# A two-layer expert network in which the first matmul runs as 26 block products in place of 28, with weight forms kept in memory and the second weight streamed

## The chip, the core and the metric

The kernel runs on one core of a Trainium2 chip. The core has a matrix engine (TensorE, PE in the profile, with the loading of its stationary operand as PEld), a vector engine (Vector, DVE), an activation engine (Scalar, ACT), a general engine (GpSimd, Pool) and a queue engine that issues transfers (SyncE, SP). Each takes its instructions in the order in which the program wrote them, and waits at one whose inputs are not ready. Sums are built in PSUM, which TensorE writes and Vector and Scalar read; all else lies in SBUF, and the inputs and outputs in DRAM. The metric is the time on the device in microseconds.

## What is computed

There are 2 sequences of 2048 tokens of width 512. First comes an adapter, then a feed-forward layer with an expert chosen per sequence. Cut to what matters (all in 32-bit floats, with the biases and both layer norms):

```python
# adapter: 512 -> 128 -> (expert 128x128, embedding) -> 512, residual, layer norm
hidden = gelu(x @ down_W.T + down_b)
hidden = hidden @ expert_W[e0].T + expert_b[e0] + domain_emb[e0]
x = layernorm(hidden @ up_W.T + up_b + x) * ln_gamma + ln_beta
# expert feed-forward: 512 -> 2048 -> 512, residual, layer norm
h = gelu(x @ Wi[e1] + bi[e1])          # Wi: 512 x 2048
r = h @ Wo[e1] + bo[e1] + x            # Wo: 2048 x 512
out = layernorm(r) * gamma[e1] + beta[e1]
```

## The kernel before

The work is cut into 8 blocks `n` of 512 tokens; blocks 0 to 3 are the first sequence, `b = 0`, and 4 to 7 the second. The program runs a block as two stages. Stage F (`f_in`, line 467) computes `h` from the adapter's transposed output `yT`; stage G (`f_out`, line 595) computes the second matmul into `x_tiles[n]`. The adapter of block n+1 is woven into G of block n by `adapter_pieces` (line 426). The program order is written by hand: `f_in` and `f_out` call `hook()` after each group of matmuls, and the lists `F[i]` and `G[i]`, filled in the loop from line 811, say which other work is put at hook i. A hook gives only the place in each engine's own queue; an engine whose queue is empty runs ahead of TensorE.

**Stage F.** Both layers use a 2x2 block scheme of seven products in place of eight (the Winograd form of Strassen's). The columns of Wi go in four tiles `d`. For each, TensorE multiplies seven forms of Wi (A11, A12, A22 and the sums S1 to S4) by seven forms of `yT` (four raw blocks, one of them replaced by a sum, and `t1`, `t2`, `t4`). A product is 4 matmuls of 128x128 by 128x256, so F has 4 x 7 x 4 = 112 (block 0 runs its first tile plainly with 32 in place of 28). Results are copied out by Scalar (`snap`, line 524), added by Vector (line 530) and passed through the gelu on Scalar (line 482). There are 28 hooks, 7 for a tile.

**Weights.** `load_wi` (line 270) loads raw Wi for the first block of a sequence, `sums_wi` (line 282) makes S1 to S4 on Pool, and `keep_wi` (line 292) writes the made tile, 1.79 MB, to DRAM; the other blocks load it from there. Two tiles are in flight. `load_wo` (line 298) loads all of Wo of a sequence at once, and `sums_wo` (line 307) makes its forms on Pool in four calls of four sums; raw Wo and the sums stay in SBUF for all four blocks.

**Stage G.** Seven products again, each of 32 matmuls over eight k; X and Y begin with six of their eight k (12 matmuls each). In hook 0 stands `a_xT` (line 442), in which Vector turns the loaded squares `xs` of the next block's x into `xT`; in hook 1 stands the adapter's first matmul, `a_down` (its matmul is line 372, tile `pdown`). Later hooks hold `a_up`, `a_norm`, the moves of 32x32 squares `ys` (line 111), the transposes into `yT` (line 447), the bias addition `a_bo` on Pool and the sums of `yT` (`a_sums`, line 412, on Vector). Sums of `h` (`h_s13`, `h_s2`, `h_s4`) run on Vector.

**The end of a block.** Layer norm of block n-1 runs in F of block n: `f_moments` and `f_rstd`, then `f_normalize` on Vector at hooks 7, 8, 14 and 15, and `f_store` three hooks later. At hook 19 `load_x` and `load_squares` fetch block n+1; there are two x buffers, so this load waits until the last store of block n-1 has landed. All these transfers are issued by SP, in order:

```python
F[7 * d + 6].append(lambda m=m: (load_wi(*m), sums_wi(*m)))
(F[7 * d + 12] if d + 1 < ND else G[5]).append(lambda m=m: keep_wi(*m))
...
F[i + 3].append(lambda s=s: f_store(n - 1, s))
...
F[19].append(lambda: (load_x(n + 1), load_squares(n + 1)))
```

Of the kernel before, what the change touches and what calls it, by code (L numbers as in the profile page):

```python
# [9 lines left out]
F32 = mybir.dt.float32  # L10
# [3 lines left out]
PSUM = bass.MemoryType.PSUM  # L14


@with_exitstack
def kernel(
# [32 lines left out]

    nc = tc.nc
    P = 128
# [21 lines left out]
    wo_pool = ctx.enter_context(tc.tile_pool(name="wo", bufs=1))  # L75
# [3 lines left out]
    pre_pool = ctx.enter_context(tc.tile_pool(name="pre", bufs=6))  # L79
    small = ctx.enter_context(tc.tile_pool(name="small", bufs=6))  # L80
    ps_x = ctx.enter_context(tc.tile_pool(name="ps_x", bufs=2, space=PSUM))
    ps_z = ctx.enter_context(tc.tile_pool(name="ps_z", bufs=2, space=PSUM))
    ps_y = ctx.enter_context(tc.tile_pool(name="ps_y", bufs=1, space=PSUM))
    ps_w = ctx.enter_context(tc.tile_pool(name="ps_w", bufs=1, space=PSUM))
    ps_a = ctx.enter_context(tc.tile_pool(name="ps_a", bufs=2, space=PSUM))

    def aux(name, pool=None, tag="aux"):
        return (pool or ps_a).tile([P, 512], F32, tag=tag, name=name)
# [175 lines left out]
    A11, A12, A22, S1, S2, S3, S4 = range(7)  # L264

    def wi_made(n, d):

        return n % BPB == 0 or (n, d) == (1, 0)

    def load_wi(n, d):  # L270
        b = n // BPB
        t = wi_tiles[n, d] = wi_pool.tile([P, 7, 2, 2 * P], F32, tag="wi", name=f"wi_{n}_{d}")
# [9 lines left out]
    def sums_wi(n, d):  # L282
        if not wi_made(n, d):
            return
# [7 lines left out]
    def keep_wi(n, d):  # L292
        b = n // BPB
        if wi_made(n, d) and (n, d) != (0, 0):
            kept = wi_kept[b, d] = dram.tile([P, 7, 2, 2 * P], F32, tag=f"wi{d}", name=f"wi_kept_{b}_{d}")
            nc.sync.dma_start(kept, wi_tiles[n, d])

    def load_wo(b):
        t = wo_pool.tile([P, NJ, H], F32, tag="wo", name=f"wo_{b}")
        src = Wo[ds(e1[b], 1)].rearrange("e (j p) h -> p (e j) h", p=P)  # L300
        for k in range(4):
            for r in range(2):
                j = r * NP + 2 * k
                nc.sync.dma_start(t[:, j : j + 2, :], src[:, j : j + 2, :])
        seq[b]["wo_raw"] = t

    def sums_wo(b, k):
        w = seq[b]
        if k == 0:
            w["wos"] = wo_pool.tile([P, 3, NP, HH], F32, tag="wos", name=f"wos_{b}")  # L310
        t, u = w["wo_raw"], w["wos"]
        lo, hi = slice(2 * k, 2 * k + 2), slice(NP + 2 * k, NP + 2 * k + 2)
        b11, b12, b21, b22 = t[:, lo, :HH], t[:, lo, HH:], t[:, hi, :HH], t[:, hi, HH:]
        t1, t2, t4 = u[:, 0, lo], u[:, 1, lo], u[:, 2, lo]
        tt = nc.gpsimd.tensor_tensor
        tt(t1, b12, b11, ALU.subtract)
        tt(t2, b22, t1, ALU.subtract)
        tt(b12, b22, b12, ALU.subtract)
        tt(t4, b21, t2, ALU.subtract)
        lo, hi = slice(0, NP), slice(NP, NJ)  # L320
        w["wo"] = dict(
            b11=t[:, lo, :HH], t3=t[:, lo, HH:], b21=t[:, hi, :HH], b22=t[:, hi, HH:],
            t1=u[:, 0], t2=u[:, 1], t4=u[:, 2],
        )
# [24 lines left out]


# [5 lines left out]
    def a_transpose(n, s):  # L356
        if s == 0:
            live["xT"] = t_pool.tile([P, NC, TB], F32, tag="xyT", name=f"xT_{n}")
        transpose_subtile(x_tiles[n][:, s, :], live["xT"], s, aux(f"pt_x_{s}", ps_z, "Z"))

    def a_down(n, lo, hi):

        xT = live["xT"]
# [3 lines left out]
        if n == 0:  # L367
            ph = aux(f"pdown_{n}_{lo}", *((ps_y, "Y") if lo % 2 else (ps_w, "W")))
        else:
            ph = aux(f"pdown_{n}")  # L370
# [9 lines left out]
    def a_up(n, s):  # L380
# [10 lines left out]
        if s == 0:  # L391
            live["mv"] = moments_tile(f"a_{n}")
# [491 lines left out]
```

## Time and profile before

| What | us |
|---|---|
| median of 3 runs (866.86, 866.91, 872.11) | 866.91 |
| the profiled execution, its own time | 865.82 |
| its span in the profile | 864.0 |
| F of block 0, from 26.0 to the first matmul of G | 52.9 |
| G of block 0 begins at | 78.9 |
| F of block 5 (552.66 to 601.0) | 48.3 |
| G of block 5 (601.0 to 656.24) | 55.2 |

The profile is of one execution. A group's line gives the line of the kernel, the engine, the operation, output and inputs by the program's names, the shapes, and how often. One matmul in 32-bit floats shows as two records of PE. The names `p..` are banks of stage F and `g..` banks of stage G. "SPq" rows are transfers being issued, not their data; the data show as the share of the 16 DMA engines and as GB/s in the windows. The transfers move 109.61 MB in the span; 104.50 MB of it are issued by SP, 4.46 MB by Scalar.

### The profile page before, as it was taken

The page shows a single profiled execution, that of the slowest core. Times are in us where ns is not written, and L with a number is a line of the kernel's source. Part 1 is how long each engine was busy: PE and PEld are TensorE (multiplying, and loading weights), DVE is VectorE, ACT ScalarE, POOL GpSimd, SP SyncE. Part 2 cuts the span into 40 slices and gives each one's busy share as a digit, 9 for nine tenths or more (in the row PEclk, how much of TensorE's full clock was granted, in tenths as well). Part 3 has the DMA queues.
Part 4 walks back from the last instruction along what each step waited for, and adds up shares of the span by engine and source line. Part 5 has one row for each costly group of instructions (what it writes and reads, how often), then busy time and mean ns, then how long its engine had stood idle before and what let it go on. Part 6 is the DMA issues. An engine that isn't in the chain of part 4 may idle for free.

```text
span 864.0 us, 10158 instructions
## 1 busy us (share of the span) xinstructions
PE 854.7 (99%) x3844; PEld 721.6 (84%) x3844; DVE 462.1 (53%) x735; ACT 193.5 (22%) x405; POOL 192.6 (22%) x160
## 2 busy tenths in 40 slices
PE   9999999999999999999999999999999999999996
PEld 6788788887888888878788878888788887888885
DVE  3735465446555374543847557454465554654325
ACT  2244003420034200441004410144002430034200
POOL 0765620020201002003426731102011020200001
PEclk9999999999999999999999999999999999999999
DMA  8965431690338602495067792059130590323001
GB/s 275 245 239 171 171 49 62 212 213 1 49 110 192 186 14 35 136 211 169 13 172 255 255 244 36 15 196 227 64 49 9 214 264 1 50 78 142 1 1 49
DMA packets 148334, 109.61 MB, mean 127 GB/s; under 512 B 120857, under 2 KB 130878, under 8 KB 144318
## 3 DMA queue, kind: packets, MB, share of 16 engines
q1 hardware_dynamic: 116972, 104.50, 41.7%
q10 hardware_dynamic: 31282, 4.46, 3.2%
q8 instruction: 30, 0.49, 0.3%
q14 instruction: 18, 0.15, 0.1%
q0 software_dynamic: 32, 0.00, 0.0%
HBM read 78.53 MB, written 23.07 MB: 118 GB/s over the span
## 4 chain that ended last, share of the span: by engine, by line
PE 99%; DVE 0%; ACT 0%; POOLq 0%; issue 0%
PE gX L462 19%; PE pX L462 19%; PE gZ L462 12%; PE pZ L462 12%; PE gW L462 6%; PE pW L462 6%; PE pY L462 6%; PE gY L462 6%; PE pup L386 3%; PE pdown L372 3%; PE pC L462 2%; PE gaux L462 1%; PE idle L751 1%; PE pup L388 0%; PE pbb L250 0%; PE pb L243 0%
## 5 line engine op out<-in xcount | busy, mean ns | idle before, releaser
L526 ACT COPY c<-pX 128x512 f32<-128x512 f32 x93 | 54.1, 582 | 423.0 <-PE pX L462 423.0
L482 ACT ACTIVATE h<-c,biT 128x256 f32<-128x256 f32 x248 | 106.1, 499 | 78.1 <-DVE c L530 78.1
L462 PE MATMUL pX<-yT,wi 128*128 128x256 f32 x496 | 117.2, 379 | 0.0
L462 PE MATMUL gX<-wo,h 128*128 128x256 f32 x512 | 114.4, 379 | 0.8 <-DVE x L620 0.8
L462 PEld LDWEIGHTS gX<-wo,h 128*128 128x128 f32 x512 | 97.2, 190 | 17.3 <-issue 3.3
L462 PEld LDWEIGHTS pX<-yT,wi 128*128 128x128 f32 x496 | 94.2, 190 | 12.8
L530 DVE TENSOR_TENSOR c<-pX,c 128x512 f32<-128x512 f32 x31 | 21.4, 692 | 123.4 <-ACT c L526 123.4
L620 DVE TENSOR_TENSOR x<-gX,x 128x512 f32<-128x512 f32 x32 | 21.3, 687 | 108.3 <-PE gX L462 108.3
L378 POOL TENSOR_TENSOR x<-x,upb 128x512 f32<-128x512 f32 x28 | 40.0, 1462 | 125.1 <-DMA x<-in_x_dram 125.1
L336 POOL TENSOR_TENSOR rstd_a<-ve_a,mhalf 128x2 f32<-128x2 f32 (+1 forms) x18 | 13.0, 723 | 227.4 <-DVE ve_a L334 226.2
L462 PEld LDWEIGHTS gX<-wos,s 128*128 128x128 f32 x256 | 48.6, 190 | 12.6 <-issue 6.7
L462 PEld LDWEIGHTS gZ<-wos,s 128*128 128x128 f32 x256 | 48.6, 190 | 12.1 <-issue 6.2
L462 PE MATMUL pZ<-yTs,wi 128*128 128x256 f32 x248 | 58.7, 379 | 0.0
L462 PE MATMUL pX<-yTs,wi 128*128 128x256 f32 x248 | 58.7, 379 | 0.0
L462 PE MATMUL pW<-yTs,wi 128*128 128x256 f32 x248 | 58.7, 379 | 0.0
L462 PE MATMUL pY<-yT,wi 128*128 128x256 f32 x248 | 58.6, 379 | 0.0
L462 PE MATMUL pZ<-yT,wi 128*128 128x256 f32 x248 | 58.6, 379 | 0.0
L462 PE MATMUL gZ<-wos,s 128*128 128x256 f32 x256 | 57.8, 379 | 0.0
L462 PE MATMUL gX<-wos,s 128*128 128x256 f32 x256 | 57.7, 379 | 0.0
L462 PE MATMUL gW<-wos,h 128*128 128x256 f32 x256 | 56.6, 379 | 0.0
L410 POOL TENSOR_TENSOR x<-x,bo 128x512 f32<-128x512 f32 x32 | 41.3, 1312 | 63.1 <-DMA ys<-x 63.1
L462 PE MATMUL gY<-wo,h 128*128 128x256 f32 x240 | 54.2, 379 | 0.0
(120 smaller groups left out, 1173.5 us busy)
## 6 DMA issues: line engine op xcount, KB each, us to landing
wi<-wi_kept SPq DMA_DIRECT2D x23, 1792.0 KB, 7.8
wi_kept<-wi SPq DMA_DIRECT2D x8, 1792.0 KB, 8.7
wo<-in_L_cond_Wo_dram SPq DMA_DIRECT2D x16, 512.0 KB, 9.7
out_dram<-x SPq DMA_DIRECT2D x32, 256.0 KB, 3.3
x<-in_x_dram SPq DMA_DIRECT2D x7, 1024.0 KB, 5.8
xs<-in_x_dram SPq DMA_DIRECT2D x28, 256.0 KB, 7.0
wi<-in_L_cond_Wi_dram SPq DMA_DIRECT2D x9, 512.0 KB, 4.6
wi<-in_L_cond_Wi_dram SPq DMA_DIRECT2D x18, 256.0 KB, 7.5
```

The lines of the kernel that those rows point to most:

```text
L336: nc.gpsimd.tensor_tensor(rstd[:, lo:hi], ve[:, lo:hi], mhalf[:, lo:hi], ALU.pow)
L372: nc.tensor.matmul(ph[:, t], dWT[:, c, :], xT[:, c, t], start=(c == 0), stop=(c == NC - 1))
L378: nc.gpsimd.tensor_tensor(x_tiles[n][:, s, :], x_tiles[n][:, s, :], seq[n // BPB]["upb"], ALU.add)
L386: nc.tensor.matmul(pu, live["hid"][:, ts(s, P)], w["up"], start=True, stop=(n > 0))
L410: nc.gpsimd.tensor_tensor(r, r, seq[n // BPB]["bo"], ALU.add)
L462: nc.tensor.matmul(bank[:, q], lhsT(k, q), rhs(k, q), start=first, stop=True, skip_group_check=True)
L482: nc.scalar.activation(h[:, j, c * HT : (c + 1) * HT], pre[:, q], AF.Gelu, bias=w["bi"][:, j : j + 1], scale=1.0)
L526: nc.scalar.copy(t, src)
L530: nc.vector.tensor_add(t, src, t)
L620: nc.vector.tensor_add(t, src, t)
L751: nc.tensor.matmul(idle[:, :P], ones, ones, start=True, stop=True, skip_group_check=True)
```

## The change

Blocks 0 and 1 keep the scheme of before (7 products of 4 matmuls for each of the four tiles, 112 in all). Blocks 2 to 7 (`n >= NW`, NW = 2) run a new `f_in_forms`: the columns of Wi go in two halves `e`, each with 26 products of two matmuls, read from a table. A product takes one of 26 forms of Wi (a 128x128 block for each of two `q`) and one form of y (128x256). It is added up in one of seven chains of PSUM banks, and after most products the running contents of the bank are added to one or two of eight results. F of these blocks has 26 hooks, one after every two products.

```diff
+PRODUCTS = (
+    (5, 3, 2, True, ((5, 1),)),
+    (4, 18, 6, True, ((5, -1),)),
+    (0, 12, 4, True, ((6, -1),)),
+    (9, 8, 3, True, ((7, 1),)),
+    (1, 20, 0, True, ((2, -1), (4, -1))),
+    (2, 11, 4, False, ((7, -1),)),
...
+    def f_in_forms(n, hooks):
...
+                for q in range(2):
+                    nc.tensor.matmul(
+                        bank[:, q], t[:, q, a, :], y[:, bb, :], start=first and q == 0, stop=True, skip_group_check=True
+                    )
+                for c, sign in adds:
+                    if c not in acc:
+                        acc[c] = [take_pre(f"c{c}_{n}_{e}"), sign]
+                        nc.scalar.copy(acc[c][0], bank)
+                    else:
...
+                            nc.vector.tensor_tensor(r, bank, r, ALU.add)
```

The forms of Wi are made by tables of sums: 39 sums of 128x128 per stage `g` (`FORMS_A`), four stages per sequence, on Pool (the first one on Vector), in one SBUF buffer that is loaded from raw Wi and written to DRAM when done. The 21 sums of y (`FORMS_B`, 128x256) run on Pool at hook 11 of G.

```diff
+    def load_stage(b, g):
+        t = live["stage"] = wi_pool.tile([P, SLOTS_A, P], F32, tag="stage", bufs=1, name=f"stage_{b}_{g}")
...
+    def stage_forms(lo, hi, engine):
+        for how in FORMS_A[lo:hi]:
+            make_form(engine, live["stage"], how)
+    def keep_stage(b, g):
...
+        nc.sync.dma_start(kept, live["stage"][:, : 2 * HALF_A, :])
...
     def a_sums(n):
...
+        if n >= NW:
+            for how in FORMS_B:
+                make_form(nc.gpsimd, t, how)
```

Wo is no longer held. Every block streams its 14 halves (128x4x256, 0.52 MB) through a ring of seven buffers: the first seven are issued in F from hook 20 (block 0), 17 (blocks 1 and 3) or 8, the rest in G as halves are used up. The sums of Wo are made in the same ring, in two calls of eight sums per sequence, and kept in DRAM.

```diff
+    def load_wo(n, i):
+        o, f = (WO_LAST if n + 1 == NB else WO_ORDER)[i]
...
+        nc.sync.dma_start(t, wo_source(b, o, f) if o[0] == "b" else wo_kept[b, o, f])
+    def raw_wo(b, f):
+        for o in ("b11", "b12", "b22", "b21"):
+            t = wo_made[o] = wo_tile(f"wo_raw_{b}_{o}_{f}")
+            nc.sync.dma_start(t, wo_source(b, o, f))
...
+    def keep_wo(b, f):
+        for o in ("t1", "t2", "t3", "t4"):
...
+            nc.sync.dma_start(kept, wo_made[o])
...
+    at(0, "F", 5, lambda: sums_wo(0, 0))
+    at(0, "F", 9, lambda: keep_wo(0, 0))
+    plan_wo(0, 0, 1, (10, 14, 19))
+    plan_wo(1, 1, 0, (1, 10, 15))
+    plan_wo(3, 1, 1, (2, 10, 15))
...
+        start = {0: 20, 1: 17, 3: 17}.get(n, 8)
+        for i in range(RING):
+            F[start + i].append(lambda i=i: load_wo(n, i))
```

`plan_wo` puts the raw loads, the sums and the writes at the three hooks named. Stage 0 of the first sequence stands in F of block 0, 1 in G of block 0, 2 and 3 in F of block 1 (sums at hooks 3 to 8 and 18 to 24, written at 10 and 27), those of the second sequence in G of block 1, F (sums at hooks 14 to 20, written at 23) and G of block 2 and G of block 3.

Around this, work is moved. For blocks from 2 on, the layer norm of the block before is split into `f_center` on Vector (hooks 10, 12, 14, 16) and, one hook later, `f_scale` on Scalar with the addition of beta on Pool; the store stands at hooks 13, 15, 17 and 19. `load_x` and `load_squares` move to hook 20 in all blocks. `a_bo` moves from G to hooks 5 to 8 of the next F. `h_s13` for the first two tiles runs on Pool at hooks 15 and 17, and `h_s3` for the other two on Pool at the start of G. G opens with four k of X and four of Y in place of six each. PSUM banks and the buffers of results are taken and given back by hand (`take_bank`, `give`) in place of fixed names.

```diff
+            first, step = ((0, 1, 3, 4), 4) if n < NW else ((2, 4, 6, 8), 8)
...
+                    F[i].append(lambda s=s: f_center(n - 1, s))
+                    F[i + 1].append(lambda s=s: f_scale(n - 1, s))
                 F[i + 3].append(lambda s=s: f_store(n - 1, s))
             if n + 1 < NB:
-                F[19].append(lambda: (load_x(n + 1), load_squares(n + 1)))
+                F[20].append(lambda: (load_x(n + 1), load_squares(n + 1)))
```

## The prediction

> **What bounds the kernel now.** I read the page first: the busy shares and the chain that ended last.
>
> ```profile
> PE 854.7 (99%) x3844; PEld 721.6 (84%) x3844; DVE 462.1 (53%) x735; ACT 193.5 (22%) x405; POOL 192.6 (22%) x160
> ...
> PE 99%; DVE 0%; ACT 0%; POOLq 0%; issue 0%
> ```
>
> TensorE is the whole chain. The waits of PE sum to 2.7 us, so there is nothing to win but matmuls, and every new wait is paid in full. Next, the chain in order of time (start, duration, matmul records; a matmul here is two records):
>
> ```profile
> 497.42 5.18 PE gX L462 x24
> 502.60 5.18 PE gY L462 x24
> 507.78 3.46 PE pdown L372 x8
> ...
> 601.00 5.18 PE gX L462 x24
> ```
>
> 24 records in 5.18 us make 0.432 us per matmul. G of one block to G of the next takes 103.58 us, of which F is 112 x 0.432 = 48.3 us. The adapter's `pdown` starts 10.36 us after G does. Then the queues that feed PE. The transfer queue around the same G (start, time in issue):
>
> ```profile
> 582.56 0.33 SPq L730 DMA_DIRECT2D out_dram<-x  x1
> 586.86 0.40 SPq L136 DMA_DIRECT2D x<-in_x_dram  x1
> 587.31 8.34 SPq L109 DMA_DIRECT2D xs<-in_x_dram  x4
> 595.75 5.61 SPq L274 DMA_DIRECT2D wi<-wi_kept  x2
> ```
>
> The last store of the old block must land (4.3 us) before `x` of the next block can be loaded. The windows show what the loads then take (PE, PEld, DVE, ACT, POOL busy, clock, DMA share, GB/s):
>
> ```profile
> 590.00:592.00 2.00, 2.00 (x11) 1.74 (x11) 0.00 (x0) 1.61 (x4) 0.00 (x0) 1.00 1.11 357
> 594.00:596.00 2.00, 2.00 (x11) 1.77 (x10) 1.97 (x2) 0.79 (x3) 2.00 (x2) 1.00 1.65 124
> 598.00:600.00 2.00, 2.00 (x11) 1.74 (x11) 0.01 (x1) 0.59 (x1) 0.39 (x1) 1.00 1.52 180
> 604.00:606.00 2.00, 2.00 (x11) 1.76 (x10) 2.00 (x4) 0.00 (x0) 0.00 (x0) 1.00 1.08 459
> ```
>
> `x` and the squares `xs` hold all engines of the DMA until 600.2, 13.3 us after the issue of `x`; two Wi tiles (3.67 MB) then take 8.3 us. Vector turns `xs` into `xT` here:
>
> ```profile
> 604.60 1.28 DVE L587 TENSOR_TENSOR s<-s,h 128x512 f32<-128x512 f32 x2
> 605.80 2.36 DVE L123 STREAM_TRANSPOSE xT<-xs 128x1024 f32<-128x1024 f32 x2
> ```
>
> So today xs lands 5.6 us before Vector turns to it, and `xT` (608.2) is done 3.2 us before `pdown` asks for it (601.0 + 10.36 = 611.4): 8.8 us of margin in all. Last, Pool and SP in block 0, where weights are made (in brackets the idle time before and what ended it):
>
> ```profile
> 67.89 1.27 POOL L287 TENSOR_TENSOR wi<-wi 128x512 f32<-128x512 f32 x1 [4.12 <-DMA wi<-in_L_cond_Wi_dram]
> 71.70 1.72 POOL L290 TENSOR_TENSOR wi<-wi 128x512 f32<-128x512 f32 x1
> 73.38 1.72 POOL L316 TENSOR_TENSOR wos<-wo 128x512 f32<-128x512 f32 x1
> 77.62 1.27 POOL L319 TENSOR_TENSOR wos<-wo,wos 128x512 f32<-128x512 f32 x1
> ```
>
> ```profile
> 73.44 0.34 SPq L296 DMA_DIRECT2D wi_kept<-wi  x1
> 74.03 0.37 SPq L278 DMA_DIRECT2D wi<-in_L_cond_Wi_dram  x1
> ```
>
> SP does not go past a write whose Pool sums are unfinished: the write of a made Wi tile leaves when L290 ends at 73.4, and the next load right behind it. G of block 0 starts at 78.9 with Wo long in place. This is the reader's key to the change: SP is one queue in order, and so is Pool.
>
> **What is removed.** F of blocks 2 to 7 goes from 112 matmuls to 2 x 26 x 2 = 104: 48 matmuls x 0.432 = 20.7 us, all on the path.
>
> **Inside the new F.** Each product is 0.86 us, and 19 of 26 reuse a chain's bank, at the nearest three products on, so evacuation has 1.73 us. The 29 additions of a half are 8 ACT copies (0.58 each) and 21 Vector adds (0.69): 14.5 us of Vector beside 22.4 us of PE, with moments (0.9) and centering (0.8) put between them. One such step and two adds is 2.3 us, over the 1.73 only where all meet at one bank. No row shows it; bounds are 0 and 8 us over six blocks (0.035 at each of 228 reuses), and I take 0.5, because the adds now wait for PE and not PE for them. The 21 sums of y move from Vector (four of 0.7) to Pool: 128x256 has no row; between 0.63 (half of the 1.27 row) and 1.27, I take 0.70. `yT` is ready 3.8 us before F (652.5 against 656.2), the ninth sum is then done at F+2.5, its product is due at F+5.2: no cost up to 0.98 us each. Wi: two tiles and up to seven Wo halves, 7.1 MB, of which 5.5 stand before the later tile, go in 14 us at 390 GB/s, 21.6 are there: nothing. The bias adds moved from G's end to F on Pool are asked for only in G, a whole F later, and leave Pool free for the sums of y. `h_s3` and two of the four `h_s13` go to Pool: 1.3 us each, the former asked for some 40 us into G. Scaling moves to ACT (0.6 a tile) and Pool (1.3), and costs in time of the store, below. SP issues 112 Wo loads where it issued 16; at 0.4 us each that is 45 us spread over 860, and in G, one half of 0.52 MB (1.4 us) per 3.45 us of PE is hidden.
>
> **Wo in block 0.** Wo is no longer resident. On SP, `keep_wo(0,1)` (hook 19) stands before the load of Wi tile (1,0) and the first Wo half (hook 20), and waits for Pool's `sums_wo(0,1)`, which stands behind `sums_wi(0,3)`. That tile can land no earlier than 67.9, since its load still follows the write of the tile before. Then 5.5 us of sums as now, and eight Wo sums in place of four: 10.2 (at 1.27) to 11, so 83.6 to 84.4. Then one kept half, Wi (1,0) and the wanted half: 2.9 MB, 7.4 us at the 390 GB/s (3.67 MB from 58.2 to 67.6), and 1 to landing: 92.4. PE wants it at 78.9. **13.5 us** (10 to 18).
>
> **Block 1.** Pool gets two stages of 39 sums of 128x128, a size with no row. Bounds are 0.32 (a quarter of the 1.27) and 0.70 (the 128x2 row of `rstd_a`); nearest is the same operation at 128x512, so I take 0.40, the quarter and most of an empty Pool instruction (0.10). Times from the start of this F: `rstd` ends at 8 as now (664.2 against 656.2 in block 6); 34 of the sums (13.6) and four bias adds (5.0) follow on Pool, to 26.6. SP holds `keep_stage` until then, and behind it the load of Wi tile (1,3): 4.4 for the keep's data, 0.7 a store, 4.6 the tile, 1 to landing and 0.5 of issue make 37.8. PE asks for it at 3/4 of 48.3, 36.2: 1.5 of stall. `sums_wo` (10.2) ends at 36.8, and keep_wo waits for it; behind keep_wo on SP stand two stores, three Wo halves, block 2's Wi tile, and only then `x`. On the DMA, the second stage's load and keep_wo last until 44.8, stores and one half until 47.6, the store lands at 49, but two halves and the Wi tile (7 us) still run until 54.7: `x` and `xs` (12 without the latency) end near 66.7, the first of two transposes at 68. `pdown` is asked for earlier than now, because G opens with two halves of 16 records (6.9 us) where it had two of 24 (10.36): 49.8 + 6.9 = 56.7. That is 11. Together **12** (5 with sums at 0.32 and the DMA at 459 GB/s, 17 at 0.70).
>
> The Trainium skill (GPSIMD Engine Reference, "3. Performance versus the Vector engine") gives a two-input add on that engine about 2.6 cycles per element plus a dispatch, 4497 ns for 2048 elements, and so speaks against cutting the sums into small pieces; with the trace's 1.27 us for 512 an estimate is 2.1 ns per element and 0.46 us for 128x128. By it block 1 would lose some 2 us more, and the sum would be 889.
>
> **Blocks 2 to 6.** Times again from the start of F, which is now 44.9 long. The last quarter of the old block is scaled at hook 17 (PE at 31.1, then ACT 1.2, Pool 1.3: 33.7). Its store stands on SP behind a Wi load that leaves when PE frees the buffer (39 products, 33.7) and moves 1.7 MB for 4.2. So the store is issued at 34.2 and lands between 38 (4.3 as now) and 40.5 (behind the Wi data); today `x` has left by 34.2 (586.9 - 552.7) of a longer F. From the issue of `x`, 13.3 to the end of `xs` and 1.3 for a transpose give 52.6 to 55.1; `pdown` is due at 44.9 + 6.9 = 51.8. That is 0.8 to 3.3; I take 2 for each of blocks 4, 5, 6: **6** (0 to 12). In block 2, 17 stage sums (6.8) stand before the last bias add on Pool, which ends near 37.5: **4** (1 to 8). In block 3 keep_wo, two halves, a row and a Wi tile stand before that store: `x` leaves near 46.7, F with its folds (3.7, from 107.3 against 103.6 now) ends at 48.6, and with 13.3 + 1.3 against 6.9 it would be 5.8: **5** (1 to 9).
>
> The granted clock is 1.00 in every window. The skill (TensorE: Matmul & The Clock Gate, Part 1) says that about 3.4 us of idling halves the clock until as much activity has passed. No wait in this trace is long enough to show it; by that rule the two longest waits would cost some 2 us more each, and the sum would be 891.
>
> **Sum.** 865.8 (profiled execution) - 20.7 + 0.5 + 13.5 + 12 + 6 + 4 + 5 = 886.1. The median of the runs lies 1.1 above that execution: 887.
>
> **Rivals.** (a) PE stays gapless: 866.9 - 20.7 = 846, up to 858. For it: in steady state the DMA has the time (share 0.25 in a G, 0.64 in an F). Its one mechanism is that the first Wo half is in place when PE asks for it at 78.9; its price is the 13.5 above, and it decides if Pool ends `sums_wo(0,1)` by 70, while the tile that stands before it lands at 67.9. It needs the later waits hidden by the same slack. Chance 0.15. (b) The waits are there but about half: block 0 at 10, block 1 at 7, the others at 1 each come to 22: 868, no change. For it: small Pool sums or faster writes. Chance 0.20. (c) Evacuation decides: 0.2 us at each of 19 reuses x 2 x 6 adds 46, so near 930. Against: Vector has 8 us free per half. Chance 0.05. (d) It skips fewer matmuls than it says: the loops are plain, 52 per half; no chance given. The forecast has 0.60.
>
> About 1%, 8.7 us, is what a measurement of this kernel can tell from no change. Faster 0.15; within 0.20; slower 0.60 + 0.05. The range must take in (b) and leave at most 0.2 out. At its top, the upper ends for blocks 0 and 1 (4.5 and 5 more), and for blocks 2 to 6 (14 more) would be 910 together; 908 leaves 0.06 above, (c) among it. At its bottom 857 leaves 0.14, nearly all of (a), below. The forecast's own range is 876 to 908.
>
> **What would show it.** Right: about 96 PE records fewer; G of block 0 starts some 13 us late, its first `gX` waiting for a DMA into `wo`; `pdown` waits for `xT` in blocks 1 to 6, longest in block 1; SP waits on Pool's Wo sums and stage sums. Wrong: PE without idle at 79, or long waits of `pF` matmuls on Vector or on Pool's sums of y.

## The result and the profile after

The changed kernel took 946.22 us (median of four runs, 942.77 to 948.37) against 867.18 before: 1.089 times as long, 95% interval 1.084 to 1.095. The prediction had 887 with a range to 908: the direction was right, the size was not. The profiled execution took 947.94 us with a span of 946.1. In its page, the first lines are busy time, share and records of each engine; the next is the granted clock in 40 slices of the span, in tenths; the last the chain that ended last, by engine:

```profile
PE 868.0 (92%) x3748; PEld 716.3 (76%) x3748; DVE 532.8 (56%) x853; ACT 207.8 (22%) x429; POOL 481.2 (51%) x596
...
PEclk9899799978899989999899998999999998999999
...
PE 58%; DMA 15%; POOL 9%; SPq 9%; DVE 4%; issue 3%; ACT 1%; POOLq 0%; DVEq 0%; ACTq 0%
```

The 96 records fewer are the 48 matmuls. But PE, which had been 99% of the chain, now shares it with transfers, Pool and SP, and its busy time has grown by 13 us though it does less (some 5 of them ahead of block 0): some of it ran at a lower clock. The waits of PE, which summed to 2.7 before, are led by these (us in total, times, longest):

```profile
PE pdown L505 <- DVE xT L196: 40.2, 6, 11.3
PE gX L601 <- DMA wo_b<-in_L_cond_Wo_dram: 10.9, 1, 10.9
PE pX L601 <- DMA wi<-wi_kept: 10.0, 1, 10.0
PE pF L724 <- DVE c L736: 4.6, 1, 4.6
PE pX L601 <- ACT c L666: 2.4, 1, 2.4
```

Cutting PE's timeline at the first matmul of each stage (a wait goes to the stage that it holds up) gives the stages' lengths in us:

| block | F before | F after | G before | G after | waits in F, G after |
|---|---|---|---|---|---|
| 0 | 52.9 | 57.4 | 55.2 | 69.2 | 2.9, 10.9 |
| 1 | 48.3 | 60.8 | 55.2 | 69.3 | 10.0, 11.3 |
| 2 | 48.3 | 45.7 | 55.2 | 63.4 | 0, 5.3 |
| 3 | 52.1 | 56.2 | 55.6 | 63.7 | 5.1, 5.4 |
| 4 | 48.3 | 45.4 | 55.2 | 64.2 | 0, 6.9 |
| 5 | 48.3 | 45.4 | 55.2 | 63.0 | 0, 4.9 |
| 6 | 48.4 | 45.5 | 55.2 | 64.1 | 0, 6.4 |
| 7 | 48.3 | 45.4 | 56.0 | 56.2 | 0, 0.8 |

The scheme itself does what it says: F of blocks 4 to 7 is 2.9 us shorter. It is paid for in G of every block but the last, and in blocks 0, 1 and 3. The stages lose more than their waits: G of block 2 is 8.2 longer with 5.3 of wait. The windows around that wait show the rest (PE, PEld, DVE, ACT, POOL busy, then the granted clock, DMA share, GB/s):

```profile
344.00:346.00 2.00, 0.01 (x1) 0.01 (x1) 1.31 (x2) 0.00 (x0) 2.00 (x2) 0.61 0.76 319
344.46:351.28 6.82, 5.29 (x7) 2.20 (x8) 2.37 (x2) 0.00 (x0) 6.64 (x6) 0.50 0.99 357
350.00:352.00 2.00, 2.00 (x4) 0.73 (x3) 0.00 (x0) 0.00 (x0) 1.10 (x1) 0.68 0.96 389
352.00:354.00 2.00, 2.00 (x10) 1.65 (x9) 0.00 (x0) 0.69 (x1) 0.00 (x0) 1.00 0.99 390
```

While PE waits (until 345.99), its clock falls to a half, at 344.46, and it stays there until 351.28, through the next 5.3 us of work. The group of `pdown` matmuls carries the same mark (busy time and mean ns of a record; idle time before): 29.3 us and 478 ns before, and now

```profile
L505 PE MATMUL pdown<-xT,dWT 128*128 128x512 f32 (+1 forms) x88 | 44.5, 666 | 40.2 <-DVE xT L196 40.2
```

One case of that wait, in block 5, in the timelines of SP and then of Vector and PE (start, time, in brackets the idle time before):

```profile
662.23 0.34 SPq L967 DMA_DIRECT2D out_dram<-x  x1
669.30 0.39 SPq L209 DMA_DIRECT2D x<-in_x_dram  x1
669.73 8.08 SPq L182 DMA_DIRECT2D xs<-in_x_dram  x4
```

```profile
682.53 2.37 DVE L196 STREAM_TRANSPOSE xT<-xs 128x1024 f32<-128x1024 f32 x2 [5.21 <-DMA xs<-in_x_dram]
```

```profile
683.83 6.35 PE L505 MATMUL pdown<-xT,dWT 128*128 128x512 f32 x8 [4.88 <-DVE xT L196]
```

The last store is issued, `x` must wait 7.1 us until it has landed, the squares stand behind `x`, arrive 13.2 us after its issue, and `pdown` starts 4.9 late and runs 6.35 where this view has 3.60 for it without a wait (run 17, below).

### The profile page after: what moved, and what is told of

It reads as the page before. It is cut to its first block, busy times and chain, and to the rows that moved or that the text cites. A ratio compares the mean times of both kernels' runs of the same rounds, so it can differ in the third digit from the quotient of the medians.

```text
span 946.1 us, 11122 instructions
## 1 busy us (share of the span) xinstructions
PE 868.0 (92%) x3748; PEld 716.3 (76%) x3748; DVE 532.8 (56%) x853; ACT 207.8 (22%) x429; POOL 481.2 (51%) x596
## 2 busy tenths in 40 slices
DMA packets 206375, 189.64 MB, mean 200 GB/s; under 512 B 123721, under 2 KB 178798, under 8 KB 204526
## 4 chain that ended last, share of the span: by engine, by line
PE 58%; DMA 15%; POOL 9%; SPq 9%; DVE 4%; issue 3%; ACT 1%; POOLq 0%; DVEq 0%; ACTq 0%
PE pF L724 19%; PE gX L601 14%; PE gZ L601 10%; SPq L182 6%; PE gW L601 5%; DMA xs<-in_x_dram 5%; DMA out_dram<-x 4%; PE pdown L505 4%; PE gY L601 3%; POOL stage L386 3%; PE pup L519 2%; POOL wo_t L440 2%; DMA forms_kept<-stage 1%; DMA stage<-in_L_cond_Wi_dram 1%; DMA wi<-in_L_cond_Wi_dram 1%
## 5 line engine op out<-in xcount | busy, mean ns | idle before, releaser
L724 PE MATMUL pF<-yT,wi 128*128 128x256 f32 x1248 | 276.4, 382 | 5.3 <-DVE c L736 4.6
L724 PEld LDWEIGHTS pF<-yT,wi 128*128 128x128 f32 x1248 | 236.5, 191 | 44.5 <-DVE c L736 6.0
L386 POOL TENSOR_TENSOR stage<-stage 128x128 f32<-128x128 f32 x266 | 143.0, 561 | 69.1 <-DMA stage<-in_L_cond_Wi_dram 61.9
L386 POOL TENSOR_TENSOR yT<-yT 128x256 f32<-128x256 f32 x126 | 88.2, 728 | 70.1 <-DVE yT L202 67.3
L739 DVE TENSOR_TENSOR c<-c,pF 128x512 f32<-128x512 f32 x96 | 65.4, 681 | 51.5 <-PE pF L724 35.7
L601 PE MATMUL gX<-wo_b,h 128*128 128x256 f32 x256 | 60.8, 393 | 10.9 <-DMA wo_b<-in_L_cond_Wo_dram 10.9
L734 DVE TENSOR_TENSOR c<-pF,c 128x512 f32<-128x512 f32 x96 | 63.9, 686 | 10.9 <-PE pF L724 9.1
L601 PEld LDWEIGHTS gX<-wo_b,h 128*128 128x128 f32 x256 | 50.7, 198 | 21.7 <-issue 14.6
L841 DVE TENSOR_TENSOR x<-gX,x 128x512 f32<-128x512 f32 x32 | 21.3, 686 | 79.1 <-PE gX L601 79.1
L778 POOL TENSOR_TENSOR h<-h 128x512 f32<-128x512 f32 x24 | 35.7, 1497 | 52.1 <-DVE s L774 51.2
L601 PE MATMUL gY<-wo_b,h 128*128 128x256 f32 x256 | 57.9, 379 | 0.0
L601 PE MATMUL gZ<-wo_t,s 128*128 128x256 f32 x256 | 57.8, 379 | 0.0
L601 PE MATMUL gX<-wo_t,s 128*128 128x256 f32 x256 | 57.7, 379 | 0.0
```

What stands on the lines that cost most here:

```text
L386: engine.tensor_tensor(t[:, d, :], t[:, x, :], t[:, y, :], ALU.add if op == "+" else ALU.subtract)
L601: nc.tensor.matmul(bank[:, q], lhsT(k, q), rhs(k, q), start=first, stop=True, skip_group_check=True)
L724: nc.tensor.matmul(bank[:, q], t[:, q, a, :], y[:, bb, :], start=first and q == 0, stop=True, skip_group_check=True)
L734: nc.vector.tensor_tensor(r, bank, r, ALU.add)
L739: nc.vector.tensor_tensor(r, r, bank, ALU.subtract)
L778: engine.tensor_tensor(a21, a11, a21, ALU.subtract)
```

## The experiments

Single executions of these kernels differ in the start: the work ahead of F of block 0 is alike in all, and took 25.8 to 31.3 us, with the clock low in part of it where it was long (26.0 in the profile of before, 31.1 in that of after). So beside each time stands **T**, the span less the start of F of block 0: 838.0 before, 915.0 after. Each T is of one execution, so a difference of 2 or 3 us in it says little by itself. The theory at the start was that the orders of SP and Pool cost the time, by waits that also halve the clock. Its rival was that the added bytes (189.64 MB against 109.61) are late in whatever order. A second rival came up on the way: Vector and Pool hold each other up.

**1. The squares ahead of x.** They need no x buffer, so they need not stand behind the store.

```diff
-                F[20].append(lambda: (load_x(n + 1), load_squares(n + 1)))
+                F[0].append(lambda: load_squares(n + 1))
+                F[20].append(lambda: load_x(n + 1))
```

> The squares of the next block are loaded at hook 0 of F instead of hook 20; x itself stays at hook 20. Order theory (the time went into transfers that stand behind others, each wait followed by some 3 us of TensorE at half clock): the waits of pdown for xT in blocks 1 to 6 (40.2 us) go to under 5 in sum, pdown falls from 6.2 to 3.5 us in those blocks, and the time falls from 946 to about 892. Load theory (190 MB in place of 110 are too much for the transfer engines, so a wait only moves): the waits come back at pF for a Wi tile or at gX for a half of Wo, and the time stays above 930.

898.99 us, T 871.4: 43.6 less, with the same 189.64 MB (about 892 us had been expected). The longest waits that are left, ahead of 4.9 for `c` in block 0 and 4.5 in block 3:

```profile
PE gX L601 <- DMA wo_b<-in_L_cond_Wo_dram: 11.0, 1, 11.0
PE pX L601 <- DMA wi<-wi_kept: 9.0, 1, 9.0
PE pup L519 <- DVE x L523: 5.1, 2, 3.0
```

`pdown` no longer waits and its busy time is back at 29.4. `x` is as late as ever, but only the residual needs it. G of blocks 4 to 6 is 55.2 as before. So more than half of the 77 us was an order, not bytes.

**2. Wo's sums ahead of a Wi tile's**, on Pool in block 0: `plan_wo(0, 0, 1, (10, 14, 19))` becomes `(10, 12, 19)`.

> In block 0 the second call of Wo sums stands at hook 12 on Pool, ahead of the sums of Wi tile 3, in place of hook 14. Order theory: Pool, idle from 59 to 73, makes them there, the write leaves about 10 us sooner, and the wait of the first gX (10.9 us) and its slow first half (6.7 for 3.6) go: 946 to about 932. Load theory: the wait is for the data of Wi tile and Wo half behind it, and at least 7 us of it stay: above 940.

942.8 us, T 914.3, where after has 915.0: neither expectation holds, since the wait for Wo fell from 10.9 to 2.9 and the time stayed. Another wait took its place:

```profile
PE pX L601 <- ACT c L666: 11.2, 2, 7.6
...
PE gX L601 <- DMA wo_b<-in_L_cond_Wo_dram: 2.9, 1, 2.9
```

Vector, which makes the first stage of forms there, fell behind. Eight sums of 128x128 in its timeline take, in the changed kernel, first beside Pool's sums of weights and then while Pool waits for the next tile (idle from 59.27 to 72.98):

```profile
52.04 7.91 DVE L386 TENSOR_TENSOR stage<-stage 128x128 f32<-128x128 f32 x8
...
61.20 1.95 DVE L386 TENSOR_TENSOR stage<-stage 128x128 f32<-128x128 f32 x8
```

and in this run, where Pool's Wo sums now fill that gap:

```profile
66.67 8.64 DVE L386 TENSOR_TENSOR stage<-stage 128x128 f32<-128x128 f32 x8
```

About 1.0 to 1.1 us each beside Pool against 0.24 alone. The Trainium skill (SBUF — State Buffer, "Who interferes with whom") says that a Vector instruction with two inputs in SBUF contends with a GpSimd instruction that reads SBUF; the rows agree, and give it a price. The additions `c`, with one operand in PSUM, keep their 0.69 us beside Pool.

**3. PE kept busy through the wait.** Matmuls on a constant, into an unused bank, stand before `pdown` in blocks 1 to 6; they add work and take none away.

```diff
+        if n >= 2:
+            at[1].append(lambda: pe_fill(n, 50 if n == 2 else 24))
```

> Idle matmuls are put before pdown: 24 (about 5 us) in blocks 2 to 6, 50 (about 11 us) in block 1, nothing else changes. Clock theory: TensorE does not stand still any more, the granted clock stays at 1.00 there and pdown takes 3.5 us in place of 6.2 in six blocks, so 946 falls to about 932 (930 to 938). Rival (pdown is slow because its operand comes late or the transfer engines are busy): pdown keeps 6 us and the time is the same or up to 6 us longer.

934.12 us, T 904.6, as expected. The data come about as late as before, but

```profile
L505 PE MATMUL pdown<-xT,dWT 128*128 128x512 f32 (+1 forms) x88 | 29.6, 481 | 1.6 <-DVE xT L196 1.6
```

14.9 us of `pdown`'s busy time are gone and 10.4 of T (some filling ran past the arrival). So the clock after a wait is a cost of its own, and doing useless work removes it.

**4 and 5. Block 1's write of a stage.** `keep_stage(0, 2)` moves from hook 10 to 13, behind the load of Wi tile (1,3); then also the one form of a stage with a turned sign, which always ran on Vector, goes to Pool.

```diff
-    at(1, "F", 10, lambda: keep_stage(0, 2))
+    at(1, "F", 13, lambda: keep_stage(0, 2))
```

```diff
-        if op == "n":
+        if op == "n" and engine is nc.gpsimd:
+            engine.tensor_tensor(t[:, d, :], t[:, x, :], t[:, y, :], ALU.add)
+            engine.tensor_scalar(t[:, d, :], t[:, d, :], -1.0, None, ALU.mult)
+        elif op == "n":
```

> In block 1 the write of the third stage stands at hook 13, behind the load of Wi tile 3, in place of hook 10 ahead of it. Queue theory: the tile's load leaves when TensorE frees its buffer near 182 and not at 193.4, the wait of pX (10.0 us) goes with its slow start: 946 to about 934. Rival (two blocks at one place: Vector stands from 190 to 207 at the sign-changing form of the next stage, which waits for Pool): TensorE goes on for a few products and then waits for the banks that Vector has not read, so that less than 5 us are won.

> The keeping of stage (0,2) stays at the later place (938.6 us with that alone) and the form with the turned sign is made by Pool (a sum and a product by -1) in place of Vector. If Vector's blocked stretch at L384 is what took the place of the wait for Wi, the wait for ACT's c (9.6 us in the run before) falls below 3 us and the whole to 925 to 931 us (9.6 less 2, and 2 to 4 of slow clock). If Vector is late anyway, because its small sums run beside Pool's, the wait stays above 6 us and the time at 935 or over.

Run 4 took 938.59 us (T 905.6): the wait for Wi went and one of 9.6 for `c` came, because Vector stood at that sign form. It does so in the changed kernel too:

```profile
207.28 0.53 DVE L384 SCALAR_TENSOR_TENSOR stage<-stage 128x128 f32<-128x128 f32 x1 [16.88 <-POOL stage L386]
```

The form needs a sum that Pool makes behind the other work of its queue, and everything behind it on Vector waits. With it on Pool (run 5), F of block 1 is 48.5 without a wait, but the time was 944.78 (T 911.8), against 925 to 931 expected: PE now reaches G earlier than the data do.

```profile
PE pdown L508 <- DVE xT L196: 40.3, 6, 11.2
PE gX L604 <- DMA wo_b<-in_L_cond_Wo_dram: 17.4, 2, 11.2
```

The second wait for Wo (6.2) and the longer one for `xT` in block 1 (11.2 against 6.2) are what block 1's later loads cost when nothing ahead of them waits any more. A miss, and a pattern: in blocks 0 and 1 three waits stand one behind the other, and removing one shows the next.

**6 and 8. All four edits; then also the stages elsewhere** (none in F of block 0, two in G of block 0, one in F and two in G of block 1; Wo's sums in F of block 1 come earlier too).

> All four edits: the squares' loads at the start of F, the first Wo sums at 12, the later keeping, the sign on Pool. From the run with early squares alone (899.0): 9.0 of wait for Wi and some 3 of slow clock go, the Wo sums change nothing (their own run), so 885 to 889. If the waits only change place again (Vector's c late beside Pool), it stays at 895 or over.

> As the run with all four edits, with the stages laid elsewhere: none beside Vector's work in F of block 0, the first two in G of block 0, one in F and two in G of block 1. If the remaining loss is the place of the stages, the waits of block 0 and 1 come to under 12 us and the time to 856 to 866 (867 less 20.7, and 10 to 20 of waits with their clock). If Vector's sums are late beside Pool wherever the stages lie, it is 875 or over.

896.84 us (T 867.2) and 906.48 (T 874.5), both misses: in T the first is only 4.2 better than early squares alone, the second 3 worse. In blocks 4 to 7 next to nothing waits; in blocks 0 to 3 it moves about: 10.7 for ACT's `c` in the first, 13.1 for Wo and 7.2 for Wi in the second.

**7, 9 and 16. The ring without the scheme.** `NW = NB`: 28 products in every block, no stages, Wi kept as before, Wo through the ring; then also early squares; then also an early request for Wo in block 0. This last edit has three lines:

```diff
-        for o in ("b11", "b12", "b22", "b21"):
+        for o in ("b11", "b22", "b21", "b12"):
...
-    plan_wo(0, 0, 1, (10, 14, 19))
+    plan_wo(0, 0, 1, (10, 12, 18))
...
-        start = {0: 20, 1: 17, 3: 17}.get(n, 8)
+        start = {0: 15, 1: 17, 3: 17}.get(n, 8)
```

Three of the seven buffers hold raw halves that are not kept. They are free when Pool's sums end, and with this order they are the first to be asked for, ahead of the copies to DRAM.

> The scheme of 28 products for every block, no forms kept, Wo through the ring as in the changed kernel. If the ring itself is cheap and the order of x behind the squares is what costs, pdown's waits for xT are under 4 us in all and the time is 867 plus the wait for Wo in block 0 (11 plus 3 of clock): 878 to 886. If the ring's traffic delays x and Wi whatever the order, pdown's waits are over 15 us and the time is 895 or over.

> The ring alone (916.5 us: 28 products for every block, no forms) with the squares' loads moved to the start of F. If the ring's own cost is the wait for Wo in block 0 and the rest of its 916.5 is the order of x behind the squares, pdown's waits go (17.6 us, and some 12 of slow clock after them, and the 3.6 before pup): 879 to 886. If the ring's traffic holds x back in whatever order, it stays at 895 or over.

> 28 products for every block, Wo through the ring, squares early and block 0's Wo asked for early. If the scheme is worth its matmuls in blocks 4 to 7 with the rest equal, this is 11 to 14 us above the run with 26 products there: span 874 to 878, ratio 1.011 to 1.018. If the stages of forms cost in blocks 1 to 3 what the products save, the two are within 4 us.

916.51 us (T 887.1), 892.6 (861.6) and 879.12 (846.9; 1.010 times before, 1.007 to 1.014). So the ring alone, in the order of the changed kernel, costs 49 us: 25.5 of it the squares behind `x`, 14.7 the order of Wo in block 0, 8.9 what is left. The first of these runs was 30 above the top of its expectation, because late squares make PE wait with the old F too, up to 9.4 in block 4. The second was 7 above its own, the third just below. Of the 8.9, F of block 0 holds 3.3 (56.2 against 52.9) and G of block 1 holds 4.4 (59.6 against 55.2).

**10 and 14. 26 products in blocks 4 to 7 alone** (`NW = 4`), so that the first sequence needs no stages; early squares, the sign on Pool. Run 10 has the early request for Wo, run 14 the old one.

> The scheme of 26 products in blocks 4 to 7 alone (no stages of the first expert), squares at the start of F, and in block 0 the first halves of Wo asked for as soon as Pool's Wo sums are done, ahead of the kept copies. Worth 32 matmuls x 0.432 = 13.8 us against before. If what costs is the work packed into blocks 0 and 1 and the order of the loads, 853 to 864, waits of TensorE under 8 us in all. If the ring or the forms cost by their traffic, 875 or over.

> The run with 26 products in blocks 4 to 7 and early squares (span 863.4), with block 0's Wo asked for as the changed kernel asks for it. If the wait for Wo in block 0 is a matter of order alone, it comes back as 11 to 14 us with 2 to 3 of slow clock: span 876 to 880 from a prologue of 26. If the bytes decide, G of block 0 stays under 60 and the span under 868.

867.77 us (0.999 times before, 0.996 to 1.002; T 837.1), 4 us over its range, and 884.49 (T 851.7), as expected. PE's waits in the second:

```profile
PE gX L605 <- DMA wo_b<-in_L_cond_Wo_dram: 14.0, 1, 14.0
```

In the first, no `gX` waits for a transfer. Its SP asks for the halves at 69.69 (43.4 us into F) and only then writes the kept ones, where the changed kernel, second, asked at 92.89 (61.8 us into F):

```profile
69.69 4.16 SPq L428 DMA_DIRECT2D wo_b<-in_L_cond_Wo_dram  x3
73.89 0.98 SPq L454 DMA_DIRECT2D wo_kept_t<-wo_t  x2
```

```profile
89.09 0.32 SPq L450 DMA_DIRECT2D wo_kept_t<-wo_t  x1
89.67 0.93 SPq L358 DMA_DIRECT2D wi<-in_L_cond_Wi_dram  x1
...
92.89 3.48 SPq L424 DMA_DIRECT2D wo_b<-in_L_cond_Wo_dram  x4
```

Two pairs differ in this order alone (14 and 10; 9 and 16), by 14.6 and 14.7 in T. Two pairs differ in the scheme in blocks 4 to 7 (9 and 14; 16 and 10), by 9.9 and 9.8: that is what it nets, of 13.8 in matmuls, with the stages that make its forms.

**11. The early request for Wo with all stages** (run 8 and the three lines).

> The re-planned stages (906.5 us) with block 0's Wo asked for early, as in the run above. If the wait for Wo in block 0 is a matter of SP's order, 13 of wait and 2 to 3 of slow clock go: 889 to 893. If Wo comes late because the bytes do, 902 or over.

908.46 us, T 880.7: a miss, 6.2 above run 8. The wait at the start of G went, and one of 8.4 inside it came. Pool's timeline shows why:

```profile
108.38 18.20 POOL L389 TENSOR_TENSOR stage<-stage 128x128 f32<-128x128 f32 x37
126.54 0.73 POOL L465 TENSOR_TENSOR rstd_a<-ve_a,mhalf 128x2 f32<-128x2 f32 x1
```

The adapter's `rstd_a`, 0.73 us long, stands behind 37 sums; Vector waits for it for 13.5 us with the addition queued that empties PE's bank.

**12, 13, 15 and 17. What is left in run 10** (waits of 1.9 for Wi in block 0 and 5.7 for `xT`). Run 12 moves Wo's sums and the ring forward in blocks 1 and 3 and a Wi copy back in block 0; run 13 does so in block 1 only and gives Vector the sums of Wi tile (0,3), with its load ahead of the copy; run 15 keeps only the latter and asks for three ring halves later:

```diff
-        tt = nc.gpsimd.tensor_tensor
+        tt = (nc.vector if (n, d) == (0, 3) else nc.gpsimd).tensor_tensor
...
+                F[20 if m == (0, 3) else (7 if n < NW else 6) * d + 6].append(lambda m=m: sums_wi(*m))
...
+            F[start + i + (3 if n in (1, 3) and i > 3 else 0)].append(lambda i=i: load_wo(n, i))
```

> The run with 26 products in blocks 4 to 7 (span 863.4 us) with the order of loads mended where its trace still shows waits: in block 0 the third Wi tile's copy to DRAM goes behind the load of the fourth tile (F of block 0: 57.2 us against 52.9 before); in blocks 1 and 3 Wo's sums and the ring's loads go earlier, and in blocks 1 and 2 a stage's loads later, so that x does not share the DMA with them (waits for xT of 3.3, 0.5 and 1.9 us, with slow clock 6.5 in all). If order and traffic are what is left, 4 and 5 us go: span 853 to 857, ratio to before 0.983 to 0.990. If the bytes are late in whatever order, the waits only change place: span 860 to 865, ratio 0.995 or over.

> As the first run with 26 products in blocks 4 to 7 alone (span 863.4), with three edits: the fourth Wi tile of block 0 is loaded ahead of the third one's copy to DRAM and its sums are made by Vector, so that Pool's Wo sums are not ahead of them; Wo's sums and ring loads of block 1 go earlier as in the run before (there F and G of block 1 took 105.0 in place of 107.1); block 3's Wo sums stay where they were, and only its stage's loads go one place later. If the waits left are each a matter of one queue's order: F of block 0 falls from 57.2 to 53 to 55, block 1 by 2, block 3 by 1, span 855 to 860 from a prologue of 26, ratio 0.988 to 0.996. If Vector's sums beside Pool's hold up TensorE's evacuations instead, F of block 0 stays at 57 or over and the ratio is 0.997 or over.

> The run with 26 products in blocks 4 to 7 (span 863.4, ratio 0.999) with the fourth Wi tile of block 0 loaded ahead of the third one's copy and its sums on Vector, and in blocks 1 and 3 the last three halves of the ring asked for after x. If each wait is one queue's order: F of block 0 54 in place of 57.2, G of block 1 56 to 57 in place of 58.8, G of block 3 56 to 57 in place of 57.7; span 857 to 860, ratio 0.991 to 0.997. If they only change place: ratio 0.998 to 1.004.

877.69 us (1.009 times before, 1.006 to 1.013), 869.08 (1.000, 0.997 to 1.002) and 864.52 (0.994, 0.992 to 0.996); T 845.7, 843.5 and 834.2. Runs 12 and 13 missed their ranges, and run 15 met its own. Run 12 shut SP in front of block 3's unfinished Wo sums, with the next Wi tile behind them (a wait of 5.8). Run 13 mended block 0 (54.1 for F in place of 57.2) and lost more in blocks 1 and 2 (219.0 in place of 211.4). Run 15 has block 0 at 53.6 and 55.2, but G of blocks 1 and 3 still 59.5 and 57.9 with `pdown` waiting for `xT`, whose squares had long landed. Vector and Pool there, in run 15:

```profile
188.57 1.67 DVE L782 TENSOR_TENSOR h<-h 128x512 f32<-128x512 f32 x1
190.16 3.42 DVE L802 TENSOR_TENSOR s<-s,h 128x512 f32<-128x512 f32 x2
193.51 1.23 DVE L196 STREAM_TRANSPOSE xT<-xs 128x1024 f32<-128x1024 f32 x1
```

```profile
188.42 6.28 POOL L517 TENSOR_TENSOR x<-x,upb 128x512 f32<-128x512 f32 x4 [22.21 <-DMA x<-in_x_dram]
```

Late `x` sets Pool's additions beside Vector's sums of `h`, which then take 1.7 us in place of 0.69, and the transposes stand behind them. Run 17 puts the transposes first:

```diff
         mul(X, a11, "b11", 0, True)
+        for f in hooks["pre"]:
+            f()
         h_s13_last(n)
         h_s2(n, 0)
...
-        at[0].append(lambda: (a_xT(n), a_residual(n)))
+        at["pre"] = [lambda: a_xT(n)]
+        at[0].append(lambda: a_residual(n))
```

> As the run before with ratio 0.994 (span 862.5 from a prologue of 28.3), with the two transposes into xT put on Vector ahead of the last sums of h at the start of G, in all blocks. If the waits for xT that are left (2.3, 0.4 and 2.0 us, with slow clock behind them 6.3 in all) come from Vector being held up by adds that run slowly beside Pool's, they go: G of blocks 1 to 3 at 55.2 to 56, span 855 to 857 from that prologue, ratio 0.985 to 0.989. If the data of x are late, they stay, and the ratio is 0.993 or over; so too if Vector's sums of h, now later, keep gZ waiting.

858.44 us (six runs, 857.02 to 859.96): **0.988 times before, 0.986 to 0.991**, T 827.0, as expected. It moves 181.48 MB, where before moves 109.61 and takes longer, so the added bytes were not late as such. The chain is PE's again, and PE starts `pdown` without a wait:

```profile
PE 96%; DVE 1%; issue 1%; DMA 1%; ACT 0%; POOLq 0%; POOL 0%; ACTq 0%; DVEq 0%
```

```profile
193.46 3.60 PE L509 MATMUL pdown<-xT,dWT 128*128 128x512 f32 x8
```

The sums of `h` are still slow there (1.38 to 1.71 each); only nothing waits for them.

From the changed kernel to this one, T falls by 43.6 (squares ahead of `x`, run 1), 19.7 (no stages for the first sequence, whose blocks 2 and 3 go back to 28 products, with the sign on Pool: run 14), 14.6 (order of Wo, run 10), 2.9 (run 15) and 7.2 (transposes, run 17), from 915.0 to 827.0. The 2.9 is the least sure of these: the ratios to before, 0.999 in run 10 and 0.994 in run 15, have intervals that just touch.

## Why the prediction was wrong

The places were right, and named: Wo late in block 0, Wi and `xT` in block 1, `xT` in blocks 2 to 6, 96 records fewer. Two terms failed. The clock behind the waits was put at nothing and cost some 26 us; the waits were put at 40.5 us in all and came to 68.6, 28 more. Those two are nearly all of the 57 by which T missed. In us of T, which is 77.0 longer (the last column sums to 76.4; the rest is spread over blocks 2 and 7):

| term | predicted | measured |
|---|---|---|
| matmuls | -20.7 | -20.7 (records counted) |
| inside the new F | 0.5 | 3.0 (six times 45.4 - 44.9) |
| block 0, Wo | 13.5 | 14.0 (10.9 wait, 3.1 clock) |
| block 0, F | 0 | 4.5 (2.4 wait, 2.1 behind it) |
| block 1 | 12 | 26.6 (21.3 wait, 5.3 clock) |
| block 2 | 4 | 8.2 (5.3 wait, 2.9 clock) |
| block 3 | 5 | 15.1 (10.5 wait, the rest mostly clock) |
| blocks 4 to 6 | 6 | 25.7 (18.2 wait, 7.5 clock) |

- **The clock, left at zero.** This is the step that failed outright: "No wait in this trace is long enough to show it", so the sum went without it. T's 77.0 and the 20.7 saved, less 68.6 of new waits (the table's, against 1.3 before) and 3.0 inside F, leave some 26 us. The profile gives most of that directly. In ten stretches the granted clock is 0.50 behind a wait, from 67.98 to 71.39 in block 0 to 791.60 to 798.43 in block 6. Windows cut to these ten sum to

```profile
sum 78.50, PE 45.93 PEld 25.80 DVE 23.48 ACT 2.69 POOL 26.68; mean PE 4.59 PEld 2.58 DVE 2.35 ACT 0.27 POOL 2.67
```

PE worked for 45.93 us at half the clock, which by estimate lost half of that, 23.0. The rule of the Trainium skill (TensorE: Matmul & The Clock Gate, Part 1) was read with "the two longest waits"; "some 2 us more each" was about right, but not two waits paid it: all nine of 4.6 us and more did, 2 to 3 us each, and the 2.4 in block 0. Even the prediction's own waits of 4 and 5 us in blocks 2 and 3 were longer than the 3.4 us of that reading. Run 3 shows the cost by taking it away.
- **"So the store is issued at 34.2 and lands between 38 and 40.5."** Issued it was, at 35.7; `x` left at 42.8 (669.30 - 626.51). The 7.1 us to landing were sized from 4.3 in a quiet kernel to 6.3. From there the step held: 13.2 to the squares (13.3 taken), 1.3 for a transpose, `pdown` due 7.1 into G (6.9 taken). The wait of 4.9 where 2 was taken is the later issue and that landing.
- **"1.5 of stall" for Wi tile (1,3)** was 10.0. SP stood behind the stage sums until 192.52, 34.8 us into F in place of 26.6. `rstd` ended at 9.7 in place of 8; the 33 sums behind it took 19.4 us in place of 13.6 (0.46 us each in the median, 0.59 on average, for 0.40 taken, where the estimate from the Trainium skill's GPSIMD Engine Reference, "3. Performance versus the Vector engine", had said 0.46); the four bias additions took 6.0 in place of 5.0. That Vector would stand in front of the sign form was not seen at all.
- **Two terms came out by luck.** Wo in block 0 cost 14.0 for 13.5, but the wait was 10.9: the data came 68.3 us into F (66.4 taken) and PE came 57.4 us into it (52.9 taken), and 3.1 of clock filled the gap. The wait for `xT` in block 1 was 11.3 for 11, because PE and `xT` both came some 11 us late.
- **Vector beside Pool.** The prediction gave Vector "8 us free per half" and counted Pool's new sums on Pool alone. In blocks 0 and 3 they slow Vector's, and PE waits 4.6 us for `c` in block 3 and 2.4 in block 0. In block 3 the three small operations that stand in front of that `c` took 4.0 us beside Pool; in the kernel before, with Pool idle, the same three took 0.28, 0.35 and 0.33 (from 375.28):

```profile
431.78 1.32 DVE L294 TENSOR_SCALAR eff<-ident,cols 128x128 f32<-128x128 f32 x1
433.14 1.37 DVE L295 SCALAR_TENSOR_TENSOR eff<-ew,cols,eff 128x128 f32<-128x128 f32 x1
434.43 1.34 DVE L297 SCALAR_TENSOR_TENSOR ebias<-eb,flags 1x128 f32<-1x128 f32 x1
```

No run moved this work away, and Vector's share of the rest of blocks 0 and 3 was not taken apart.
- Of the rivals, the evacuation (c) has a trace of truth, 0.5 us a block in place of 8. Its sign, a long wait of `pF` on Vector, showed once, by the slowed operations in block 3. (a) needed every wait hidden, and (b) the waits at about half. Run 17 comes within 3 us of the gapless sum for the scheme in four blocks (838.0 - 13.8), but by changes of order that the diff does not have.

What stays open is why the stages of the first sequence cost 19.7 more than the 6.9 that the products they serve save. Set beside each other, runs 1 and 14 say where: run 1 is 6.5 longer in F of block 0, 13.1 in F of block 1 and 5.1 in F of block 3, and the other stages come to 5 less. Runs 6, 8 and 11 name waits that the stages cause (Vector beside Pool, `rstd_a` behind them, Wi), but no run took each alone.

## What to carry to other kernels

Where TensorE has no slack, price each new wait twice, once for the wait and once for the clock behind it, and multiply by the number of waits. Before adding transfers to a queue kept in order, list what stands behind each blocking entry, and pull ahead whatever does not need what it waits for: the squares behind `x` were 43.6 us of the 77 and two lines. The raw Wo halves behind the kept ones were 14.6 and three lines in the kernel without the first sequence's stages; with them, in run 11, the same three lines won nothing, as another wait stood behind the first. Work put on an idle Pool is not free: it delays short operations queued behind it (0.73 us behind 18.2), and it slows a Vector that reads two operands from SBUF (0.24 us to 1.0).

## What was not expected of the hardware

The cost of the clock does not follow the wait's length. In run 10 `pdown` waited 3.28 us (194.19 to 197.47) and then took 3.70; in run 15 it waited 2.29 (192.50 to 194.79) and took 5.40. In all 19 profiles the granted clock changes only at steps of 3.41 us, and cut at these steps, the windows around the two waits read, run 10 first:

```profile
192.21:195.62 3.41, 1.98 (x10) 1.40 (x8) 3.41 (x3) 0.00 (x0) 3.41 (x3) 1.00 1.07 446
195.62:199.03 3.41, 1.56 (x4) 0.85 (x5) 2.92 (x3) 0.00 (x0) 0.09 (x1) 1.00 0.98 346
```

```profile
191.74:195.15 3.41, 1.12 (x5) 0.63 (x4) 3.41 (x4) 0.00 (x0) 2.97 (x2) 1.00 1.01 425
195.15:198.56 3.41, 3.41 (x5) 1.35 (x4) 0.71 (x1) 0.00 (x0) 0.00 (x0) 0.50 1.05 312
```

The longer wait fell into two steps, with PE idle for 1.4 and 1.9 us of them, and cost no clock; the shorter one fell into one step, idle for 2.3 of its 3.41, and the next step ran at half. From block 0 to the last matmul this holds in all 19 profiles: a step at full clock in which PE was idle for 2.0 us or more was always followed by one at 0.50, and one with less than 1.9 never; between the two, four of five were. The Trainium skill (TensorE: Matmul & The Clock Gate, Part 1) says that the window in which activity is counted runs freely and does not start with the work; the rows agree with that. They do not agree with the prediction's reading of the page, 3.4 us of idling: 2.3 us inside one step were enough. In these runs a wait of 2.3 to 3.3 us cost 0.2 to 2 us more.

A Vector sum of two SBUF operands is slowed by Pool's 128x512 additions fourfold at 128x128 (0.24 to 1.0 us) and two and a half times at 128x512 (0.69 to 1.7). The transposes, with one operand, took 1.20 to 1.24 us each beside Pool as without it.
